# Three row tiles transposed by VectorE from squares loaded from DRAM, a last pair finished in pieces, and a mask check moved to a later stage

## The chip, the cores and the metric

The kernel runs on one core of one Trainium2 chip. The metric is the device time of one execution in microseconds (us), of which lower is better. A core has five engines that run beside each other: TensorE (PE in the profile; matmuls, with PEld for its weight loads), VectorE (DVE), ScalarE (ACT), GpSimd (POOL) and SyncE (SP, which here only issues DMAs). Sixteen DMA engines move data between DRAM and the core's memory (SBUF); matmuls write to another memory, PSUM.

## The reference

The input x has 4 x 512 = 2048 rows of 1024 numbers (fp32). Two layers follow each other, and each ends with a residual sum and a layernorm over the row:

```python
attn = einsum('ds,td->st', w1, w2) * sparse_mask      # 1024 x 1024, mostly zero
x = layernorm(x + gelu(einsum('bds,st->bdt', x, attn) + b2))
w_l, w_h = dequant(qweight, lut4, 4 bits), dequant(qweight, lut8, 8 bits)
y = where(norm(x) > 64, x @ w_h.T, x @ w_l.T) + bias
x = layernorm(x + y)
```

The mask of this input has ones only within 70 columns of the diagonal. After the first layernorm a row's norm is about 32, so the 8 bit weights are not needed for this input. The kernel relies on both facts, but checks them on the chip: it counts rows above 64 and blocks of the mask with something outside the band, and if the count is above zero a general path (lines 42 to 189) computes everything anew. With this input that path doesn't run.

## The kernel before, in words

The 2048 rows are 16 row tiles of 128 (numbered 0 to 15). A tile's `x` lies in SBUF as 128 partitions x 1024 and is overwritten step by step with the results. The stages:

1. **Product of w1 and w2**, only in the band (L451), while the 4 bit weights are unpacked by VectorE, ScalarE and GpSimd (L293 to L344, in steps that are spread between other work). The unpacked weight is transposed by TensorE (`transpose_pending`) into `wT`, with the identity added, so that the residual sum of the second layer is part of its matmul.
2. **Attention of a row tile n** (`attention`, L529). TensorE transposes x in 8 blocks of 128 x 128 (`transposed`, L478, by `transpose_blocks`, L276; ScalarE copies each half from PSUM, L282), multiplies with the band of `attn` (`band_rows`, L507), VectorE adds b2 (z, L533), ScalarE takes the Gelu (L534), VectorE adds x and sums the row (L538). Then the layernorm: VectorE makes the negative mean `nm` (L377), ScalarE the sum of squares (`junk`, L380), GpSimd the reciprocal root r (L382, L383), VectorE normalizes (L387). The normalization is put into a list `later` and written out by the next call of `now()`, so that other work stands between.
3. **Second layer of tiles 0 to 3**, in two halves of 512 columns (`left` and `right`, `ffn_half`, L590): 8 matmuls of 512 columns each (L552), then `combine` (L564) adds the bias and sums the row.
4. **Second layer of tiles 4 to 15 in six pairs** (`ffn_pair`, L659), by a scheme with 7 instead of 8 block products. Each product is 4 matmuls of 512 columns (L669) into one of the PSUM banks u, v, w. Its inputs are tiles transposed by another way: VectorE transposes each 32 x 32 square (`squares`, L615), a DMA writes them to DRAM (`there`), four DMAs read them back in the other order (`rows`), and ScalarE, VectorE and GpSimd make copies, sums and differences (`pair_inputs`, L635). The combined weights t1 to t4 are made by `weight_sum` (L613, 2.28 us each) after each `right` half.

The order of work is the list `todo` (L720 to L727): attention 0 to 3, then `left` 0 to 3 alternating with attention 4 to 7, attention 8 to 11, then `right` 0, attention 12, `right` 1, attention 13 and so on, then the pairs. What is prepared for the next entry (its transposed tile) is written one entry ahead (L765). A scheduler orders the instructions of each engine at build time, except that VectorE keeps the written order from attention 8 on (L755). Each engine then runs its own list strictly in order, and waits for others by semaphores. All DMAs of this part are issued by SP, in order.

Three details matter for the change. `check_outside` (L488) loads the part of a block of mask rows that is outside the band into a buffer of the tag `z` (two buffers, shared with the attention's z and the outputs) and lets ScalarE sum the absolute values (L495); it is called for 8 blocks from attention 9 and `left` 2 on, which the scheduler puts between 111 and 199 us. `count_odd` (L703) and `count_all` (L713) make the count after pairs 0 and 1. And the tiles 12 to 15 are loaded (L760 to L762) when the memory of the unpacking stage is free.

Of the kernel before, what the change touches and what calls it, by code (L numbers as in the profile page):

```python
# [9 lines left out]
FP = mybir.dt.float32  # L10
# [3 lines left out]
AF = mybir.ActivationFunctionType  # L14
ALU = mybir.AluOpType
AX = mybir.AxisListType

P = 128
D = 1024
SOON = 12  # L20
PAIR = 2
KT = D // P
HALF = 512
NH = D // HALF
EPS = 1e-5
# [5 lines left out]
SQ = 32  # L31
Q = P // SQ
EARLY = 4
# [3 lines left out]
def window(s):  # L37

    return max(0, s * P - BAND), min(D, (s + 1) * P + BAND)
# [153 lines left out]
def kernel(  # L193
# [21 lines left out]
    with ExitStack() as main:  # L215
# [172 lines left out]

        x_tiles = []

        def load_x(pool, n):
            t = pool.tile([P, D], FP, tag=f"x{n}", name=f"x{n}")
            nc.sync.dma_start(out=t, in_=x[ts(n, P), :])
            x_tiles.append(t)

        attn = band.tile([P, KT, WIN], FP, name="attn")

# [79 lines left out]

        def transposed(n, tag, bufs, by_bit):  # L478
            xT = late.tile([P, KT, P], FP, tag=tag, name="xT", bufs=bufs)
            if by_bit:  # L480
                cols = x_tiles[n].rearrange("t (b s) -> t s b", s=8)
                transpose_blocks(xT, lambda k: cols[:, k, :])
            else:
                transpose_columns(xT, x_tiles[n])
            return xT


        def check_outside(s):  # L488

            lo, hi = window(s)  # L490
            raw = work.tile([P, D], FP, tag="z", name="raw", bufs=2)
            for i, (a, b) in enumerate(((0, lo), (hi, D))):
                if a < b:
                    nc.sync.dma_start(out=raw[:, a:b], in_=sparse_mask[ts(s, P), a:b])
                    nc.scalar.activation(  # L495
                        raw[:, a:b], raw[:, a:b], AF.Abs, accum_out=outside[:, 2 * s + i : 2 * s + i + 1]
                    )

        def band_rows(xT):
            ps = ps_mm.tile([P, D], FP, tag="mm", name="mm")  # L500
# [73 lines left out]
        def finish_rows(n):  # L574
            y = x_tiles[n]
            total = work.tile([P, 1], FP, tag="total", name="total", bufs=4)
            nc.vector.tensor_tensor(total, sums[:, n, 0:1], sums[:, n, 1:2], ALU.add)
            nm, r, _ = stats(y, total)

            def rest():  # L580
                if n < EARLY:
                    o = last.tile([P, D], FP, tag="o", name="o")
                else:
                    o = work.tile([P, D], FP, tag="z", name="o", bufs=2)
                normalize(o, y, nm, r)
                nc.sync.dma_start(out=out[ts(n, P), :], in_=o)

            later.append(rest)

# [45 lines left out]
        def pair_inputs(pool, n, top, low):  # L635


            def halves(tag):
                both = late.tile([P, KT, P], FP, tag=tag, name="halves")
                return both, both[:, :KH, :], both[:, KH:, :]  # L640

            def by_squares(block):
                return block.rearrange("p k (a r) -> p k a r", a=Q)


            side = (n - EARLY) // PAIR % 2
            (a1, a11, a12), (_, s1, s2), (_, s3, s4) = (
                halves(f"early{2 * i + side}") for i in range(3)
            )
            a22 = pool.tile([P, KH, P], FP, tag="a22", name="a22", bufs=2)  # L650
            nc.scalar.copy(by_squares(a1), top)  # L651
            nc.vector.tensor_tensor(by_squares(s1), low[:, :KH], low[:, KH:], ALU.add)  # L652
            nc.vector.tensor_tensor(by_squares(s3), top[:, :KH], low[:, :KH], ALU.subtract)
            nc.scalar.copy(by_squares(a22), low[:, KH:])
            nc.gpsimd.tensor_tensor(s2, s1, a11, ALU.subtract)  # L655
            nc.gpsimd.tensor_tensor(s4, a12, s2, ALU.subtract)
            return a11, a12, a22, s1, s2, s3, s4

        def ffn_pair(pool, n, blocks, between):  # L659

            a11, a12, a22, s1, s2, s3, s4 = blocks
            t1, t2, t3, t4 = (weights[i] for i in range(1, 5))
            u = pool.tile([P, HALF], FP, tag="u", name="u", bufs=2)
            v = pool.tile([P, HALF], FP, tag="v", name="v", bufs=1)
            w = pool.tile([P, HALF], FP, tag="w", name="w", bufs=1)

            def times(ps, a, b, start, stop):
                for k in range(KH):
                    nc.tensor.matmul(  # L669
                        out=ps,  # L670
                        lhsT=a[:, k, :],
                        rhs=b[:, k, :],
                        start=start and k == 0,
                        stop=stop and k == KH - 1,
                        skip_group_check=True,
                    )

            left, right = bias_bc[:, :HALF], bias_bc[:, HALF:]
            y11, y12 = x_tiles[n][:, :HALF], x_tiles[n][:, HALF:]
            y22 = x_tiles[n + 1][:, HALF:]  # L680
            times(u, a11, b11, True, False)
            nc.vector.tensor_tensor(y11, u, left, ALU.add)
            now()
            between(0)
            times(w, s1, t1, True, False)
            nc.vector.tensor_tensor(y22, w, right, ALU.add)
            between(1)
            times(u, s2, t2, False, False)
            nc.vector.tensor_tensor(y12, u, right, ALU.add)  # L689
            times(w, s4, b22, False, True)  # L690
            combine(n, 1, w, y12)
            times(u, s3, t3, False, False)
            combine(n + 1, 1, u, y22)
            between(2)
            times(v, a12, b21, True, True)
            combine(n, 0, v, y11)
            finish_rows(n)
            times(u, a22, t4, False, True)
            combine(n + 1, 0, u, left)
            now()  # L700
            finish_rows(n + 1)

        def count_odd():  # L703

# [21 lines left out]
        unpack_after = [("attention", 1), ("left", 0), ("attention", 4), ("left", 1)]  # L726
        unpack_after += [("attention", 5), ("left", 2), ("attention", 6), ("left", 3)]  # L727

        kept = {}
        rows, blocks = {}, {}  # L730

        def prepare_pair(n, part):

            if n == NT:
                return
            if part < PAIR:
                rows[n + part] = squares(last, n + part)
            else:
                blocks[n] = pair_inputs(last, n, rows[n], rows[n + 1])

        def prepare(what, n):
            if what == "attention":
# [3 lines left out]
            return kept[n]  # L746

        ready = prepare(*todo[0])
        checks = 0
        ordered = main.enter_context(ExitStack())  # L750
        for i, (what, n) in enumerate(todo):
            if (what, n) == ("left", 0):
                transpose_pending(0)
            if (what, n) == ("attention", 2 * EARLY):
                ordered.enter_context(tc.manual_schedule(engines={mybir.EngineType.DVE}))  # L755
            if (what, n) == ("attention", SOON - 2):
                steps(100)
                transpose_pending(0)
                first_sb.close()
                last = main.enter_context(tc.tile_pool(name="last", bufs=1, side="right"))  # L760
                for m in range(SOON, NT):
                    load_x(last, m)  # L762
            xT = ready
            if i + 1 < len(todo):
                ready = prepare(*todo[i + 1])  # L765
            if what == "attention":
                if n >= SOON + 1:
                    attention(n, xT, lambda: prepare_pair(EARLY, n - SOON - 1))
                else:
                    attention(n, xT)  # L770
                if n < 2 * EARLY:
                    now()
                if n > 8 and checks < KT:
                    check_outside(checks)
                    checks += 1
            else:
                ffn_half(n, xT, 0 if what == "left" else 1)
                if what == "left" and n > 1:
                    check_outside(checks)
                    checks += 1  # L780
                if what == "right":
                    weight_sum(last, n + 1)
                    now()
            if (what, n) in unpack_after:
                steps(1)
        while checks < KT:
            check_outside(checks)
            checks += 1
        first_ps.close()
        ps_pair = main.enter_context(  # L790
            tc.tile_pool(name="ps_pair", bufs=1, space=bass.MemoryType.PSUM)
        )
        for n in range(EARLY, NT, PAIR):
            ffn_pair(ps_pair, n, blocks[n], lambda part, m=n + PAIR: prepare_pair(m, part))
            if n == EARLY:
                n_odd = count_odd()
            elif n == EARLY + PAIR:
                count_all(n_odd)
        now()
        ordered.close()  # L800

# [41 lines left out]
```

## Time and profile before

| | |
|---|---|
| runs | 363.34, 363.91, 362.96 us; median 363.34 |
| profiled execution | 363.37 us, span in the profile 361.6 us, mean granted TensorE clock 0.975 |
| busy over the span | PE 328.1 us (91%), PEld 200.3 (55%), DVE 230.3 (64%), ACT 165.7 (46%), POOL 96.8 (27%) |
| DMA | 43.90 MB in 28331 packets, mean 121 GB/s |
| L281 transposes of x on PE | 160 records, 22.6 us |
| L495 mask sums on ACT | 14, 7.8 us, and 14 reads of the accumulator, 2.6 us |
| L619 transposes of squares on DVE | 12, 2.03 us each |
| pairs 0 to 5 on PE, from start to start | 28.40, 25.15, 24.20, 24.91, 24.28, 24.03 us |

Times of instructions are counted from the start of the span. A line of the order in time has the start, the duration, engine, line of the code, operation, output <- inputs, the shape, and in brackets how long the engine stood before it and for whom. Instructions of one group in a row are merged (x8 for 8). A matmul of fp32 appears as two records, so 4 matmuls of 512 columns are x8 and 3.43 us from start to start. The chain of waits is followed back from the last instruction to what released each; its lines give start, duration and what ran. Matmuls are pipelined, so a busy PE isn't PE at its peak.

### The profile page before, as it was taken

The numbers are of one execution on the slowest core, as the hardware profiler recorded it, in microseconds if no ns is written. First come the engines' busy times: TensorE is split into PE (matmuls) and PEld (weight loads), VectorE is DVE, ScalarE is ACT, GpSimd is POOL, SyncE is SP. The second block draws the span as 40 slices with busy tenths as digits, with TensorE's granted clock in tenths as the row PEclk, the third lists the DMA queues.
The fourth block names the chain that finished last, engine by engine and source line by source line (L and its number), as shares of the span: only waits on it lengthen the run. The fifth ranks groups of instructions, "written<-read, shape, count | busy, mean of one in ns | idle before, by whom it ended". The sixth has DMA issues, their size and how long they took to land.

```text
span 361.6 us, 3701 instructions
## 1 busy us (share of the span) xinstructions
PE 328.1 (91%) x1216; PEld 200.3 (55%) x1216; DVE 230.3 (64%) x353; ACT 165.7 (46%) x242; POOL 96.8 (27%) x130
## 2 busy tenths in 40 slices
PE   6799989769999987999999888999999999999970
PEld 6588778637567576956665433443444434444430
DVE  1689899697987997556767953654635626644130
ACT  4794995888659876675454311202212012022011
POOL 0810550682036322231321420402203004022000
PEclk9999999969999999899999999999999999999995
DMA  8999109500101001712235215162351451522003
GB/s 253 316 325 383 67 0 355 228 0 0 47 2 44 0 3 36 284 44 101 97 123 185 94 61 171 59 214 78 140 181 30 187 160 58 203 87 117 1 4 122
DMA packets 28331, 43.90 MB, mean 121 GB/s; under 512 B 7568, under 2 KB 20624, under 8 KB 28304
## 3 DMA queue, kind: packets, MB, share of 16 engines
q1 hardware_dynamic: 26976, 43.44, 34.9%
q10 hardware_dynamic: 1328, 0.15, 0.3%
q8 instruction: 11, 0.18, 0.2%
q14 instruction: 16, 0.13, 0.1%
HBM read 28.90 MB, written 14.68 MB: 121 GB/s over the span
## 4 chain that ended last, share of the span: by engine, by line
PE 35%; DVE 27%; ACT 9%; DMA 9%; POOL 8%; issue 7%; SPq 1%; ACTq 0%; POOLq 0%; DVEq 0%
PE u L669 16%; PE w L669 8%; ACT junk L380 6%; DVE x L538 4%; PE v L669 4%; POOL root L326 4%; DVE root L331 4%; DVE e L329 4%; DMA rows<-there 3%; DVE z L533 3%; POOL r L383 3%; PE mm L552 2%; PE mm L451 2%; DMA w_raw<-in_L_attn_w_dram 2%; DVE root L335 2%
## 5 line engine op out<-in xcount | busy, mean ns | idle before, releaser
L380 ACT ACTIVATE junk<-x,nm 128x1024 bf16<-128x1024 f32 x32 | 36.7, 1148 | 67.0 <-DVE nm L377 64.7
L507 PE MATMUL mm<-attn,xT 128*128 128x198 f32 (+2 forms) x320 | 62.1, 349 | 1.6 <-DVE attn L461 1.5
L322 ACT ACTIVATE e<-v,lt,diff 128x1024 f32<-128x1024 uint8 x48 | 56.6, 1236 | 4.1 <-DVE v L297 2.6
L552 PE MATMUL mm<-wT,xT 128*128 128x512 f32 x128 | 58.4, 611 | 0.0
L507 PEld LDWEIGHTS mm<-attn,xT 128*128 128x128 f32 x320 | 53.5, 194 | 8.6 <-DVE attn L461 1.9
L326 POOL TENSOR_SCALAR root<-v,diff,lt 128x1024 f32<-128x1024 uint8 x16 | 38.2, 2397 | 50.0 <-DVE v L297 34.7
L669 PE MATMUL u<-t,halves 128*128 128x512 f32 x96 | 43.3, 594 | 1.0 <-DVE x L689 1.0
L382 POOL TENSOR_SCALAR r<-ss 128x1 f32<-128x1 f32 x32 | 10.8, 337 | 116.7 <-ACT junk L380 116.6
L552 PEld LDWEIGHTS mm<-wT,xT 128*128 128x128 f32 x128 | 24.5, 197 | 28.2 <-issue 27.9
L655 POOL TENSOR_TENSOR halves<-halves 128x512 f32<-128x512 f32 x6 | 9.5, 1586 | 84.9 <-DVE halves L652 84.9
L619 DVE STREAM_TRANSPOSE squares<-x 128x1024 f32<-128x1024 f32 x12 | 24.3, 2029 | 11.6 <-DMA there<-squares 11.6
L669 PEld LDWEIGHTS u<-t,halves 128*128 128x128 f32 x96 | 18.1, 190 | 24.7 <-issue 22.8
L651 ACT COPY halves<-rows 128x1024 f32<-128x1024 f32 x6 | 6.3, 1042 | 55.3 <-DMA rows<-there 55.3
L281 PE MATMUL pt<-ident,x 128*128 128x128 f32 x160 | 22.6, 283 | 9.4 <-ACT wT L282 7.9
L451 PE MATMUL mm<-w2T,w_sb 128*128 128x268 f32 (+1 forms) x128 | 28.9, 375 | 2.0 <-DMA w_sb<-in_L_attn_w_dram 1.6
L281 PEld LDWEIGHTS pt<-ident,x 128*128 128x128 f32 x160 | 19.4, 154 | 13.0 <-ACT wT L282 9.3
L330 DVE COPY_PREDICATED root<-v,e 128x1024 f32<-128x1024 uint8 x16 | 22.7, 1417 | 5.3 <-POOL root L326 3.1
L534 ACT ACTIVATE z<-z 128x1024 f32<-128x1024 f32 x16 | 16.9, 1056 | 20.0 <-DVE z L533 20.0
L282 ACT COPY xT<-pt 128x512 f32<-128x512 f32 x40 | 21.2, 589 | 10.6 <-PE pt L281 10.6
L451 PEld LDWEIGHTS mm<-w2T,w_sb 128*128 128x128 f32 x128 | 22.8, 189 | 5.6 <-ACT w2T L282 2.5
L387 DVE TENSOR_SCALAR x<-x,nm,r 128x1024 f32<-128x1024 f32 x16 | 13.0, 812 | 20.3 <-POOL r L383 19.0
L329 DVE COPY_PREDICATED e<-v,e 128x1024 f32<-128x1024 uint8 x16 | 22.1, 1383 | 1.8 <-ACT e L322 1.8
(74 smaller groups left out, 435.8 us busy)
## 6 DMA issues: line engine op xcount, KB each, us to landing
x<-in_L_attn_x_dram SPq DMA_DIRECT2D x16, 512.0 KB, 7.6
out_dram<-o SPq DMA_DIRECT2D x16, 512.0 KB, 2.6
there<-squares SPq DMA_DIRECT2D x12, 512.0 KB, 3.0
rows<-there SPq DMA_DIRECT2D x48, 128.0 KB, 2.9
w_raw<-in_L_attn_w_dram SPq DMA_DIRECT2D x8, 512.0 KB, 7.0
w_sb<-in_L_attn_w_dram SPq DMA_DIRECT2D x3, 1024.0 KB, 7.5
w_sb<-in_L_attn_w_dram SPq DMA_DIRECT2D x2, 512.0 KB, 7.0
raw<-_L_attn_sparse_mask_dram SPq DMA_DIRECT2D x2, 413.0 KB, 3.4
```

Source lines behind the costliest of these rows:

```text
L281: nc.tensor.transpose(pt[:, j, :], block(g * (HALF // P) + j), ident)
L282: done = nc.scalar.copy(dst[:, g * (HALF // P) : (g + 1) * (HALF // P), :], pt)
L322: nc.scalar.activation(entry[j], plane(0), AF.Identity, scale=d_k, bias=l_k)
L326: nc.gpsimd.tensor_scalar(entry[j], plane(0), d_k, l_k, ALU.mult, ALU.add)
L329: nc.vector.copy_predicated(entry[2], plane(1), entry[3])
L330: nc.vector.copy_predicated(root, plane(1), entry[1])
L380: nc.scalar.activation(junk, u, AF.Square, bias=nm, accum_out=ss)
L451: part = nc.tensor.matmul(out=ps[:, : hi - lo], lhsT=w1_sb[s][:, k, :], rhs=w2T[:, k, lo:hi], start=(k == 0), stop=(k == KT - 1),)
L507: nc.tensor.matmul(out=ps[:, a:b], lhsT=xT[:, s, :], rhs=attn[:, s, a - lo : b - lo], start=h not in fresh, stop=hi == D or (h == 0 and wi ...
L552: nc.tensor.matmul(out=ps, lhsT=xT[:, k, :], rhs=wT[:, k, ts(h, HALF)], start=(k == 0), stop=(k == KT - 1),)
L619: nc.vector.transpose(out=t, in_=x_tiles[n].rearrange("t (c j k) -> t c k j", c=Q, k=KT))
L669: nc.tensor.matmul(out=ps, lhsT=a[:, k, :], rhs=b[:, k, :], start=start and k == 0, stop=stop and k == KH - 1, skip_group_check=True,)
```

## The change

Four edits, all in the kernel's main function:

- **Tiles 13 to 15 are transposed by VectorE.** After the loads of x12 to x15, twelve more DMAs on SP (`load_squares`, four per tile) read tiles 13 to 15 a second time from DRAM, in runs of 32 numbers (128 bytes), so that every 32 x 32 square lies where it belongs in the transposed tile. They go into the memory of t3 and t4, which are written later. One transpose instruction of VectorE (L497 of the changed file) turns all squares of a tile in place of 8 transposes of TensorE and 2 copies of ScalarE. The rows of a tile are taken in another order (row 4i + a at partition 32a + i), so the loads and stores of these tiles follow it (`rows_of`).
- **The mask's rest moves to the pairs.** The loads go into the tiles 0 to 3, whose results have been stored, and are written at the start of pairs 1 to 4; the sums on ScalarE are placed behind a copy of `pair_inputs` in the preparation of pairs 2 to 5.
- **The count** moves from pairs 0 and 1 to the start of pair 5.
- **The last pair's end** (`finish_last`): the product v comes before the third u product. The layernorm of tile 14 is finished by ScalarE, which also issues its store. The last product of tile 15 comes in two pieces of 256 columns into the free banks w and v; VectorE adds each piece and takes its mean and variance with `bn_stats`; the output is normalized and stored in two halves, by SP and ScalarE.

In the built program, the transposes of tiles 13 to 15 stand on VectorE between `nm` (L377) and `normalize` (L387) of the tile before. Without the 24 transposes the lists of TensorE differ in little up to the pairs. In the pairs the scheduler places the four matmuls of v differently: before, the products ran in pair 0 as u v1 w u w u v3 u (v1 for one matmul of v), in pair 1 as u w v3 u w v1 u u, in pairs 2 and 4 as u w u w v1 u v3 u, in pair 3 as u w v2 u w v2 u u; after, in pair 0 as u v3 w u w u v1 u, in pairs 1 and 3 as u w u w v1 u v3 u, in pairs 2 and 4 as u w v2 u w v2 u u.

The diff, cut to its core:

```diff
+        def rows_of(dram, n):
+            rows = dram[ts(n, P), :]
+            return rows if n <= SOON else rows.rearrange("(i a) d -> a i d", a=Q)
...
+        def load_squares(t, n):
+            cols = x[ts(n, P), :].rearrange("(i a) d -> i (a d)", a=Q)
+            cols = cols.rearrange("i (m g j) -> g i m j", g=Q, j=SQ)
+            for g in range(Q):
+                nc.sync.dma_start(
+                    out=t[ts(g, SQ), :].rearrange("i (m j) -> i m j", j=SQ), in_=cols[g]
+                )
...
         def transposed(n, tag, bufs, by_bit):
             xT = late.tile([P, KT, P], FP, tag=tag, name="xT", bufs=bufs)
+            if n > SOON:
+                nc.vector.transpose(
+                    out=xT.rearrange("p k (a i) -> p a k i", a=Q),
+                    in_=in_squares[n].rearrange("p (a k j) -> p a k j", a=Q, k=KT),
+                )
+                return xT
...
         def check_outside(s):
-            raw = work.tile([P, D], FP, tag="z", name="raw", bufs=2)
...
+            for raw, _, _, _, i in outside_band(s):
+                nc.scalar.activation(raw, raw, AF.Abs, accum_out=outside[:, i : i + 1])
...
+            if n + PAIR == NT:
+                times(v, a12, b21, True, True)
+                combine(n, 0, v, y11)
+                finish_last(
+                    n, lambda: times(u, s3, t3, False, True), u, (w, v), a22, t4, y22
+                )
+                return
...
+        def finish_last(n, third, u, banks, a22, t4, y22):
...
+            nm, r, _ = stats(x_tiles[n], total)
+            nc.gpsimd.tensor_tensor(nm, nm, r, ALU.mult)
+            o = last.tile([P, D], FP, tag="o", name="o")
+            nc.scalar.activation(o, x_tiles[n], AF.Identity, scale=r, bias=nm)
+            nc.scalar.dma_start(out=rows_of(out, n), in_=o)
+            third()
...
+            nc.vector.tensor_tensor(y22, u, y22, ALU.add)
+            nc.vector.tensor_tensor(y[:, :HALF], u, bias_bc[:, :HALF], ALU.add)
+            for c in (2, 3):
+                statistics(c)
+            for c in (0, 1):
+                for k in range(KT // 2):
+                    nc.tensor.matmul(
+                        out=banks[c][:, :piece],
+                        lhsT=a22[:, k, :],
+                        rhs=t4[:, k, ts(c, piece)],
...
+                nc.vector.tensor_tensor(
+                    y[:, ts(c, piece)], banks[c][:, :piece], y[:, ts(c, piece)], ALU.add
+                )
+                statistics(c)
+            nc.vector.bn_aggr(mv, st)
+            r = work.tile([P, 1], FP, tag="r", name="r", bufs=4)
+            nc.vector.tensor_scalar(r, mv[:, 1:2], EPS, None, ALU.add)
+            nc.gpsimd.tensor_tensor(r, r, minus_half, ALU.pow)
+            o = work.tile([P, D], FP, tag="z", name="o", bufs=2)
+            for h, queue in ((0, nc.sync), (1, nc.scalar)):
...
+                queue.dma_start(
+                    out=rows_of(out, n + 1)[:, :, ts(h, HALF)], in_=o[:, ts(h, HALF)]
+                )
...
+                blocks[n], copied = pair_inputs(last, n, rows[n], rows[n + 1])
+                m = n - EARLY - 2 * PAIR
+                if 0 <= m < KT:
+                    with tc.issue_after(copied.ins):
+                        for s in range(m, m + PAIR):
+                            check_outside(s)
...
+                t3, t4 = (
+                    last.tile([P, 2, D], FP, tag=f"t{i}", name="in_squares") for i in (3, 4)
+                )
+                in_squares = {13: t3[:, 0, :], 14: t4[:, 0, :], 15: t4[:, 1, :]}
+                for m in in_squares:
+                    load_squares(in_squares[m], m)
...
         for n in range(EARLY, NT, PAIR):
+            m = n - EARLY - PAIR
+            if 0 <= m < KT:
+                for s in range(m, m + PAIR):
+                    load_outside(s)
+            if n == NT - PAIR:
+                count_all(count_odd())
             ffn_pair(ps_pair, n, blocks[n], lambda part, m=n + PAIR: prepare_pair(m, part))
-            if n == EARLY:
-                n_odd = count_odd()
-            elif n == EARLY + PAIR:
-                count_all(n_odd)
```

## The prediction, made before the changed kernel ran

> **What bounds the kernel now.** I read the chain of waits first, then the instructions in order of time for TensorE (PE), VectorE (DVE) and the end, then the busy time per stage. The page's summary of the chain:
>
> ```profile
> PE 35%; DVE 27%; ACT 9%; DMA 9%; POOL 8%; issue 7%; SPq 1%; ACTq 0%; POOLq 0%; DVEq 0%
> ```
>
> PE is 91% busy over the span but holds only 35% of the chain. In the stage that loses the transposes (attention 12 to 15 between the `right` halves) the chain in order of time does not touch PE at all:
>
> ```profile
> 185.40 0.81 DVE x L387
> 186.21 0.62 DVE x L564 x2
> 187.32 1.25 ACT junk L380 x2
> 188.65 0.81 POOL r L382
> 189.53 0.56 POOL r L383
> 190.16 0.69 issue
> 190.85 1.22 DVE z L533
> 192.06 1.96 DVE squares L619
> 194.02 1.13 DVE x L538 x2
> 195.44 1.25 ACT junk L380 x2
> 197.04 0.56 POOL r L383
> 197.63 0.81 DVE x L387
> ```
>
> One turn, 185.40 to 197.63, is 12.2 us of DVE, ScalarE (ACT) and GpSimd (POOL) in a ring. PE's own share of a turn, in the order of time:
>
> ```profile
> 188.18 1.04 PE L281 MATMUL pt<-ident,x 128*128 128x128 f32 x8
> 189.05 7.03 PE L552 MATMUL mm<-wT,xT 128*128 128x512 f32 x16
> 195.92 3.76 PE L507 MATMUL mm<-attn,xT 128*128 128x198 f32 x20
> ...
> 213.67 3.67 PE L669 MATMUL w<-wT,halves 128*128 128x512 f32 x8 [1.36 <-DVE x L686]
> 218.37 3.70 PE L669 MATMUL u<-t,halves 128*128 128x512 f32 x8 [1.04 <-DVE x L689]
> ```
>
> From start to start that is 0.87 + 6.87 + 3.60 = 11.34 us: PE runs ahead, and pays for it at 213.67 and 218.37, where it waits for DVE. From 218.37 to its end at 350.49 PE is nearly dense: only two waits of 1.05 (before 249.56 and 298.75). The end, all of it after PE:
>
> ```profile
> 346.89 3.60 PE L669 MATMUL u<-t,a 128*128 128x512 f32 x8
> 350.53 0.69 DVE L564 SCALAR_TENSOR_TENSOR x<-u,bias_bc 128x512 f32<-128x512 f32 x1 [2.28 <-PE u L669]
> 352.40 1.15 ACT L380 ACTIVATE junk<-x,nm 128x1024 bf16<-128x1024 f32 x1 [2.79 <-DVE nm L377]
> 354.58 0.81 DVE L387 TENSOR_SCALAR o<-x,nm,r 128x1024 f32<-128x1024 f32 x1 [2.30 <-POOL r L383]
> 355.42 0.33 SPq L586 DMA_DIRECT2D out_dram<-o  x1
> ```
>
> The last store leaves 4.93 us after PE (355.42 - 350.49), lands 3.7 us later (the DMA view), and 2.5 us of closing follow: 11.1 us.
>
> **Step 1, before the turns (144 to 162).** Removed from ACT: 14 mask sums (7.8 us with 2.6 of accumulator reads) and 6 copies of transposed blocks (0.59 each). DVE is dense from 112 to 139, so nothing is won there. PE stands from 142.24 to 144.38 and then works with a granted clock of 0.50 from 146 to 149; its work up to band 10 is the same in another order. The one place on the chain is 155.86, where four mask sums (1.09) stand ahead of the Gelu of tile 11. They go, but one copy of tile 12 (0.59), formerly done early, takes the place. Followed to `combine` of `right` 0, which PE then holds back, DVE arrives 0.4 us earlier (162.40 to 162.0). Bounds: 0 and 1.9 (no clock drop).
>
> **Step 2, the turns (162 to 200).** PE loses 3 x 0.87 = 2.6 us. DVE gains three 32x32 transposes (L497 of the changed file). No row shows them with this layout; the same instruction at L619 takes 2.03 us on the same 128x1024. In the built order they stand between `nm` and `normalize`, where DVE idles 2.31 us for r (seen before 173.18, 185.40 and 197.63). 2.03 < 2.31, so I cost them at nothing; without that cover it would be 2.03 each. What they cost for sure is PE's lead: band 15 now waits for a transpose that starts at `nm` of tile 14 (195.32 - 0.4) and ends at 197.05, so band 15 ends at 200.65 (199.52 before). Its consumer z(15) was at 203.07, so the turn stays 12.2. POOL computes r beside the transpose. If the two lock each other out, the first POOL operation starts at 2.03 instead of 1.45 us after `nm`, and r comes 0.6 later, three times: 1.8 us. L382 has a row for such a delay: 0.81 instead of 0.19 beside L613. The other bound is 0; a shorter transpose gains nothing, since r is late anyway. The nearest row, L545 at 210.52, ended at 211.07, 0.14 us into a transpose; it may have begun first and settles nothing. I take 0. [...]
>
> **The squares' loads.** 12 DMAs of 1024 runs of 128 bytes, 12,288 packets, behind x12 to x15 on SP. SP's next store comes at 167. The memory is free when PE has read the last root (142.3); 2 MB at the 380 to 430 GB/s of 146 to 150 last till about 149. The time of such packets is bounded by two rows: between 12 and 18 us the queues carried 2891 packets, 1560 of them under 512 bytes, 1.98 MB, busy 113% of 16 engines; taking the 1331 larger ones at 380 GB/s leaves 13 to 21 ns for a small one, and the page's mean over all of queue 1 is 34.9% x 361.6 x 16 / 26976 = 75 ns. I take the first, its packets being of this size: 10 to 16 us, all there by 165. DVE needs tile 13 at 170.5, 14 at 182.7, 15 at 194.9. [...]
>
> **Step 3, pairs 0 and 1.** Here PE still follows DVE, 0.4 earlier than before. Pair 0 has three v matmuls ahead of w instead of one: 200.65 + 3.43 + 2.57 + 3 x 3.43 = 216.95, then it waits for y12 (L689: 218.35 - 0.4 = 217.95), then u, one v, u: 3.43 + 0.86 + 3.43, end 225.7 (227.92 before). Pair 1 has no v early, so it waits twice: for y22 (L686, 236.9), w and v to 241.2, for y12 (L689, 242.15), then 9.43: end 251.6 (253.07 before). So DVE's chain, not PE's work, eats the 2.6 us.
>
> **Step 4, pairs 2 to 5.** A pair is 28 matmuls x 0.858 = 24.03. Pairs 2 and 4 have no v between the last two u products, where 1 and 3 lacked it before: 1.05 each, as often as before. 251.6 + 25.08 + 24.20 + 25.08 = 326.0. The mask sums (2.2 to 2.4 us a pair) fill the 2.07 us in which ACT idles between 250.40 and 252.46, and delay two statistics by up to 0.5; DVE's y12 was done at 266.16 and PE took it at 267.67, so 1.5 us cover that; without cover it would be 0.5 in each of four pairs. The mask's loads stand ahead of rows (L629) on SP, 0.4 MB or 1 us; the halves waited 4 us for use. The count's matmul moves into pair 5: before, it sat in a wait (248.61) and cost nothing; in a dense stretch I take 0.3 (0.1 to 1.0); its counts are ready 2 us before. PE ends at 326.0 + 24.03 + 0.3 = **350.3** (350.49).
>
> **Step 5, the end.** The last product comes in two 256 wide pieces, so after PE there is: add 0.42 (L564's 0.69 and L533's 1.22 give the slope), statistics of 256 about 0.4 (no row; between the 0.19 of L710 and the 0.69 of L564), aggregation and epsilon 0.55, the power 0.55 and two handovers 0.2, two halves of 512 at 0.46 and 0.54: 3.15 instead of 4.93. The mean of row tile 14 leaves DVE: its 0.81 went in between (351.14). The last store is half as large: 2.0 if it moves as fast as 512 KB did (1.4 us of data), 3.7 if what held the last store up is no matter of size; other stores took 2.6, which I take. With 2.5 of closing: 8.25, 2.9 less than before (1.2 to 3.9).
>
> **Sum.** 350.3 + 8.25 = 358.55 of span. The profiled execution took 363.37 with a span of 361.6, so 1.8 lie around it (median of the runs: 363.34): **360.3 us**.
>
> **Rivals.**
> (a) The front gets rid of the clock drop of 146 to 149, or the chain gains as much otherwise: DVE 1.9 earlier instead of 0.4, **358.8**. For it: ACT loses 14 sums. Against: the wait 142.24 to 144.38 hangs on a weight copy behind statistics, both still there. 0.15.
> (b) POOL waits for the transposes: 1.8 later, **362.1**. For: L382's 0.81. [...] 0.12.
> (c) The end gains only 1.2, since the landing stays 3.7 and the statistics are slow: **362.0**. For: the last landing was 3.7 where others of the same size took 2.6. 0.11.
> (d) Slower: the squares come late and DVE stands at the transposes of tile 15 with all behind it. At 75 ns a packet the loads end at 149 + 57.6 = 206.6 instead of 194.9: 11.7 later, **372**. It decides from (194.9 - 149) x 16 / 12288 = 60 ns. Against: the 13 to 21 ns. 0.07.
> The forecast, with 359.2 to 361.4 about it: 0.55.
>
> **Chances.** A measurement here can tell 0.3% (1.1 us) from no change. Faster than 362.25: the forecast, (a), most of (c), half of (b): 0.85. Within: the rest of (b) and (c), 0.08. Slower: (d), 0.07. The range reaches over (a), (b) and (c): 358.5 to 362.3.
>
> **What would show it.** Right: L497 begins right after `nm`, takes about 2.0, and the `normalize` behind it still waits for r; PE idles about 1.8 us before bands 14 and 15; PE's end near 350.3 although 24 transposes are gone; the last store leaves near 3.2 us after PE. Wrong: a wait on in_squares at DVE; L382 at 0.8 beside L497; PE's end below 349 (the turn was PE's after all) or above 352; a landing of 3.7.

## The result, and the profile after

The changed kernel takes 371.75 us (median of 4 runs, 370.89 to 372.43); the kernel before took 363.19 us beside it (median of 4). The ratio is 1.0242, 95% interval 1.0213 to 1.0271: **slower by 2.4%**, where 360.3 us was forecast. The profiled execution took 371.34 us with a span of 369.5. All times below are counted from the start of a profiled span.

I read the end first. The order of time of the changed kernel, from TensorE's last piece of work on (TensorE ends at 352.60):

```profile
352.63 0.42 DVE L778 TENSOR_TENSOR x<-v,x 128x256 f32<-128x256 f32 x1 [0.72 <-PE v L770]
353.09 0.43 DVE L762 BATCH_NORM_STATS2 b_bc<-x 128x6 f32<-128x256 f32 x1
354.09 0.55 POOL L785 TENSOR_TENSOR r<-r,minus_half 128x1 f32<-128x1 f32 x1 [4.72 <-DVE r L784]
354.67 1.00 DVE L788 TENSOR_SCALAR o<-x,b_bc,r 128x512 f32<-128x512 f32 x2 [0.66 <-POOL r L785]
355.24 0.56 SPq L796 DMA_DIRECT2D out_dram<-o  x1
355.70 0.55 ACTq L796 DMA_DIRECT2D out_dram<-o  x1
```

The last store leaves 3.10 us after TensorE, as forecast (3.15). But the span goes on for another 13.8 us, in which no engine computes. What happens there is in the table by stretches of the same kernel. Its columns are the stretch and its length, then busy time and number of instructions of PE, PEld, DVE, ACT and POOL, then TensorE's granted clock, the mean busy share of the 16 DMA engines, and GB/s:

```profile
356.00:358.00 2.00, 0.00 (x0) 0.00 (x0) 0.00 (x0) 0.00 (x0) 0.00 (x0) 0.50 0.27 78
358.00:360.00 2.00, 0.00 (x0) 0.00 (x0) 0.00 (x0) 0.00 (x0) 0.00 (x0) 0.50 0.27 104
360.00:362.00 2.00, 0.00 (x0) 0.00 (x0) 0.00 (x0) 0.00 (x0) 0.00 (x0) 0.50 0.26 95
362.00:364.00 2.00, 0.00 (x0) 0.00 (x0) 0.00 (x0) 0.00 (x0) 0.00 (x0) 0.50 0.25 97
```

The reader is to see the share: flat at a quarter, for a megabyte (row tiles 14 and 15). The kernel before moved most of its last 512 KB in one stretch of 2 us (share 0.70, 266 GB/s):

```profile
356.00:358.00 2.00, 0.00 (x0) 0.00 (x0) 0.00 (x0) 0.00 (x0) 0.00 (x0) 0.50 0.70 266
```

A quarter of 16 is as much as four engines can do; the view gives only the mean of the 16. The loads of tiles 13 to 15 look the same: from 146 to 162 us, in stretches of 4 us, the share is 0.28 to 0.42 at 105 to 114 GB/s, and SP's own order of time shows it held up in the issues:

```profile
144.27 25.54 SPq L408 DMA_DIRECT2D in_squares<-in_L_attn_x_dram  x12
169.91 0.78 SPq L617 DMA_DIRECT2D out_dram<-o  x1
```

The second loss lies earlier. The order of time of TensorE in the changed kernel, where it waits for ScalarE's copy of the last weights, and of two instructions of VectorE, the merge of the last weight (L335) and z of tile 7:

```profile
145.21 1.97 PE L281 MATMUL pt<-ident,x 128*128 128x128 f32 x8 [3.43 <-ACT wT L282]
```

```profile
133.65 1.31 DVE L335 COPY_PREDICATED root<-v,root 128x1024 f32<-128x1024 uint8 x1
134.85 1.21 DVE L564 TENSOR_TENSOR z<-mm,b_bc 128x1024 f32<-128x1024 f32 x1
```

The same places in the kernel before, where the wait is shorter and z (L533 there) comes first:

```profile
144.38 0.66 PE L281 MATMUL pt<-ident,x 128*128 128x128 f32 x4 [2.14 <-ACT wT L282]
133.56 1.22 DVE L533 TENSOR_TENSOR z<-mm,b_bc 128x1024 f32<-128x1024 f32 x1
134.69 1.32 DVE L335 COPY_PREDICATED root<-v,root 128x1024 f32<-128x1024 uint8 x1
```

Behind TensorE's wait its clock falls, and stays low for longer than before. The tables by stretches of the changed kernel and of the kernel before (the granted clock is third from the end):

```profile
144.00:146.00 2.00, 0.79 (x4) 0.79 (x5) 0.83 (x2) 2.00 (x5) 0.99 (x4) 0.57 0.40 147
146.00:148.00 2.00, 2.00 (x9) 1.97 (x8) 1.78 (x4) 2.00 (x5) 0.49 (x1) 0.50 0.24 96
148.00:150.00 2.00, 2.00 (x6) 1.59 (x5) 0.05 (x1) 1.68 (x4) 0.19 (x1) 0.50 0.41 131
150.00:152.00 2.00, 2.00 (x10) 1.93 (x10) 0.00 (x0) 0.00 (x0) 0.93 (x3) 0.72 0.42 109
```

```profile
144.00:146.00 2.00, 1.62 (x9) 1.52 (x10) 1.20 (x2) 2.00 (x6) 1.43 (x4) 0.91 0.94 233
146.00:148.00 2.00, 2.00 (x8) 1.65 (x8) 0.91 (x3) 2.00 (x5) 0.00 (x0) 0.50 0.97 369
148.00:150.00 2.00, 2.00 (x10) 1.90 (x10) 0.00 (x0) 1.83 (x5) 1.13 (x4) 0.74 1.03 420
```

In the fourth stretch it was 1.00 again in the kernel before. Summing (1 - clock) x 2 us gives 1.7 us of full-speed work lost before and 3.4 us after. `combine` of `right` 0 comes at 164.14 (162.40 before, 162.0 forecast).

The transposes, last, in the order of time of the changed kernel:

```profile
172.47 0.15 DVE L377 TENSOR_SCALAR nm<-total 128x1 f32<-128x1 f32 x1
172.65 1.25 DVE L497 STREAM_TRANSPOSE xT<-in_squares 128x1024 f32<-128x1024 f32 x1
174.07 0.19 POOL L382 TENSOR_SCALAR r<-ss 128x1 f32<-128x1 f32 x1 [5.97 <-ACT junk L380]
174.93 0.81 DVE L387 TENSOR_SCALAR x<-x,nm,r 128x1024 f32<-128x1024 f32 x1 [1.03 <-POOL r L383]
```

L497 starts 0.03 us after `nm`, with no wait on the squares; `normalize` behind it still waits for r. L382 starts 1.60 us after the start of `nm`, as in the kernel before (170.72 and 172.32). It does not run beside the transpose: that takes 1.25 us and ends at 173.90, 0.17 us ahead of L382. So these rows do not show whether the two would hold each other up.

From 164.14 on, the changed kernel reaches TensorE's end in 188.46 us; 350.3 - 162.0 = 188.3 was forecast. So the miss of the span (369.5 - 358.55 = 10.95) is in two places: 164.14 - 162.0 = 2.14 in the front, and 16.9 - 8.25 = 8.65 behind TensorE's end. These two and the 0.16 between them are the whole of it.

### The profile page after: what moved, and what is told of

Same layout as the page of the kernel before. It is cut to its first block, busy times and chain, and to the rows that moved or that the text cites. A ratio compares the mean times of both kernels' runs of the same rounds, so it can differ in the third digit from the quotient of the medians.

```text
span 369.5 us, 3672 instructions
## 1 busy us (share of the span) xinstructions
PE 326.5 (88%) x1200; PEld 199.3 (54%) x1200; DVE 235.3 (64%) x360; ACT 162.0 (44%) x235; POOL 96.6 (26%) x130
## 4 chain that ended last, share of the span: by engine, by line
DVE 33%; DMA 19%; PE 13%; ACT 12%; issue 8%; POOL 7%; SPq 3%; ACTq 0%; DVEq 0%; POOLq 0%
DMA rows<-there 7%; ACT junk L380 7%; DMA there<-squares 5%; DVE squares L650 5%; DVE x L569 4%; PE u L700 4%; DVE root L331 4%; POOL r L383 3%; DVE e L329 3%; DVE z L564 3%; DMA x<-in_L_attn_x_dram 2%; SPq L660 2%; PE mm L583 2%; POOL root L326 2%; DVE root L335 2%
## 5 line engine op out<-in xcount | busy, mean ns | idle before, releaser
L538 PEld LDWEIGHTS mm<-attn,xT 128*128 128x128 f32 x320 | 54.3, 197 | 13.5 <-issue 5.8
L380 ACT ACTIVATE junk<-x,nm 128x1024 bf16<-128x1024 f32 x31 | 35.6, 1149 | 58.9 <-DVE nm L377 56.5
L583 PE MATMUL mm<-wT,xT 128*128 128x512 f32 x128 | 57.5, 602 | 0.0
L382 POOL TENSOR_SCALAR r<-ss 128x1 f32<-128x1 f32 x31 | 10.5, 338 | 111.3 <-ACT junk L380 111.2
L650 DVE STREAM_TRANSPOSE squares<-x 128x1024 f32<-128x1024 f32 x12 | 24.3, 2028 | 10.8 <-DMA there<-squares 10.8
L565 ACT ACTIVATE z<-z 128x1024 f32<-128x1024 f32 x16 | 16.9, 1058 | 30.6 <-DVE z L564 30.6
L281 PE MATMUL pt<-ident,x 128*128 128x128 f32 x136 | 19.5, 289 | 9.8 <-ACT wT L282 8.3
L387 DVE TENSOR_SCALAR x<-x,nm,r 128x1024 f32<-128x1024 f32 x16 | 13.0, 812 | 17.3 <-POOL r L383 13.8
L281 PEld LDWEIGHTS pt<-ident,x 128*128 128x128 f32 x136 | 16.9, 160 | 12.7 <-ACT wT L282 9.4
L569 DVE SCALAR_TENSOR_TENSOR x<-z,x 128x1024 f32<-128x1024 f32 x16 | 21.3, 1332 | 2.7 <-ACT z L565 2.7
L700 PE MATMUL w<-wT,halves 128*128 128x512 f32 x48 | 21.7, 595 | 1.2 <-DVE x L717 1.2
```

What stands on the lines that cost most here:

```text
L281: nc.tensor.transpose(pt[:, j, :], block(g * (HALF // P) + j), ident)
L380: nc.scalar.activation(junk, u, AF.Square, bias=nm, accum_out=ss)
L538: nc.tensor.matmul(out=ps[:, a:b], lhsT=xT[:, s, :], rhs=attn[:, s, a - lo : b - lo], start=h not in fresh, stop=hi == D or (h == 0 and wi ...
L565: nc.scalar.activation(z, z, AF.Gelu)
L569: nc.vector.scalar_tensor_tensor(xt, z, 1.0, xt, ALU.mult, ALU.add, accum_out=total)
L583: nc.tensor.matmul(out=ps, lhsT=xT[:, k, :], rhs=wT[:, k, ts(h, HALF)], start=(k == 0), stop=(k == KT - 1),)
```

## The experiments

Theory **T1**: the pattern `(i a) d -> a i d` with a = 4, which tiles 13 to 15 got for loads and stores, lets only as much as four of the 16 DMA engines work on a transfer. Rivals: **T2**, ScalarE's queue is slow; **T3**, rows that lie four apart are slow. For the front, **F1**: without the mask's sums the scheduler orders VectorE's and ScalarE's work otherwise; rival **F2**: the second load or the transposes hold it up.

All runs at a glance. The first three columns are of the profiled executions: from the `combine` at 113 to 116 us (that of `left` 2) to that of `right` 0; from there to TensorE's end; from there to the end of the span. The time is the median, the ratio that to the kernel before on the same chip.

| kernel | front | turns and pairs | end | time | ratio (95%) |
|---|---|---|---|---|---|
| before | 48.47 | 188.09 | 11.1 | | |
| after | 50.75 | 188.46 | 16.9 | 371.75 | 1.0242 (1.0213 to 1.0271) |
| a_split | 50.70 | 188.31 | 9.2 | 363.99 | 1.0021 (1.0000 to 1.0042) |
| a_split_stores | 49.49 | 188.00 | 10.0 | 363.41 | 0.9992 (0.9956 to 1.0028) |
| a_sp_queue | 50.70 | 188.18 | 16.8 | 371.44 | one run |
| b_last4 | 46.89 | 188.11 | 18.2 | 369.75 | one run |
| b_last16 | 46.84 | 188.11 | 12.2 | 365.12 | one run |
| b_end | 48.16 | 188.11 | 8.3 | 360.14 | 0.9940 (0.9912 to 0.9967) |
| b_chk | 50.61 | 188.42 | 11.0 | 365.26 | 1.0072 (1.0041 to 1.0104) |
| a_plain16 | 49.48 | 192.93 | 8.3 | 366.39 | 1.0073 (1.0039 to 1.0108) |
| a_plain16_chk | 73.21 | 188.37 | 8.5 | 386.24 | 1.0668 (1.0618 to 1.0717) |
| s_root_late | 48.52 | 188.25 | 9.2 | 362.36 | 0.9961 (0.9931 to 0.9991) |
| s_root_early | 50.74 | 188.11 | 9.4 | 364.80 | 1.0024 (0.9998 to 1.0051) |
| e_root_early | 47.21 | 188.12 | 8.4 | 359.39 | 0.9903 (0.9869 to 0.9937) |

### The end: four engines, a queue, or rows far apart

**a_split** cuts every load and store of tiles 13 to 15 into four:

```diff
+                rows = rows.rearrange("(i a) d -> a i d", a=Q)
+                parts = [(rows[a], t[ts(a, SQ), :]) for a in range(Q)]
+            for r, s in parts:
...
+                queue.dma_start(out=s if into_sbuf else r, in_=r if into_sbuf else s)
...
-            nc.sync.dma_start(out=t, in_=rows_of(x, n))
+            move_rows(nc.sync, x, n, t, True)
...
-            nc.scalar.dma_start(out=rows_of(out, n), in_=o)
+            move_rows(nc.scalar, out, n, o, False)
```

> The changed kernel, with each load and each store of tiles 13 to 15 cut into four transfers of 32 partitions (32 rows of DRAM each), so that no transfer has a leading dimension of 4. Theory T1 (a transfer whose DRAM pattern leads with 4 is carried by a quarter of the DMA engines: about 100 GB/s in the trace of after, from 144 to 164 us and from 351 to 367 us): the stores land about 3 us after their issue, the span ends some 8.5 us after TensorE's end instead of 16.9, SP no longer stands from 144 to 170 us, time 361 to 363.5. Theory T2 (ACT's queue, or two queues side by side, are slow at the end): no change, 370 to 373. Theory T3 (rows of DRAM that lie four apart, or runs of 2 KB, are slow): no change, 370 to 373. The front's later combine (+1.7 us on VectorE's chain) stays under all three.

363.99 us. The end shrinks from 16.9 to 9.2 us; the same bytes to the same rows now move at a share of 0.89. The table by stretches of this kernel:

```profile
352.00:354.00 2.00, 0.89 (x5) 0.43 (x3) 1.21 (x4) 0.00 (x0) 0.00 (x0) 1.00 0.89 221
356.00:358.00 2.00, 0.00 (x0) 0.00 (x0) 0.00 (x0) 0.00 (x0) 0.00 (x0) 0.58 0.67 173
358.00:360.00 2.00, 0.00 (x0) 0.00 (x0) 0.00 (x0) 0.00 (x0) 0.00 (x0) 0.50 0.39 106
```

T1 holds, and T3 cannot carry the loss, since the rows of each part still lie four apart. The last microsecond to the 8.25 of the forecast is probably issue: ScalarE needs about 1.9 us for the last four stores and ends at 357.87, where one store alone left at 355.70. The time lies half a microsecond above the expected range.

**a_sp_queue** gives ScalarE's two stores to SP (`nc.sync` for `nc.scalar`), patterns as in the changed kernel.

> The changed kernel with ACT's two stores (tile 14, second half of tile 15) issued by SP instead, patterns unchanged. T2 (ACT's queue is what is slow): the tail after TensorE's end falls from 16.9 to about 8.5 us, time 362 to 364. T1 and T3: tail 16 to 18 us, time 370 to 373.

371.44 us, an end of 16.8: T2 falls.

**b_last4** and **b_last16** go the other way: the kernel before, with one store changed (a = 4, and a = 16 in the second; the input of the store is left as it was, so the rows of tile 15 go out in another order).

```diff
-                nc.sync.dma_start(out=out[ts(n, P), :], in_=o)
+                rows = out[ts(n, P), :]
+                if n == NT - 1:
+                    rows = rows.rearrange("(i a) d -> a i d", a=4)
+                nc.sync.dma_start(out=rows, in_=o)
```

> The kernel before, with the last store of tile 15 alone given the DRAM pattern that leads with 4 (row 4i+a instead of row 32a+i, so the rows of tile 15 go out in another order); 512 KB. T1: about 100 GB/s, 5.2 us for the bytes instead of 1.3, so the store lands 7 to 8 us after its issue instead of 3.7 and the time is 366 to 368. T2: no change (SP's queue), 363 to 364. T3: as T1, 366 to 368.

> The same with a pattern that leads with 16 (row 16i+a... of tile 15 in another order): rows just as far from each other, 16 in the leading dimension. T1: all 16 engines carry it, the store lands after 3.5 to 4 us, time 363 to 364. T2: 363 to 364. T3: as slow as the pattern that leads with 4, 366 to 368.

The pattern alone makes the old end as slow as the new one: the end is 18.2 us with 4, 12.2 with 16. The tables by stretches of b_last4 and of b_last16, where the last 512 KB move:

```profile
356.00:358.00 2.00, 0.00 (x0) 0.00 (x0) 0.00 (x0) 0.00 (x0) 0.00 (x0) 0.50 0.26 63
360.00:362.00 2.00, 0.00 (x0) 0.00 (x0) 0.00 (x0) 0.00 (x0) 0.00 (x0) 0.50 0.25 78
```

```profile
358.00:360.00 2.00, 0.00 (x0) 0.00 (x0) 0.00 (x0) 0.00 (x0) 0.00 (x0) 0.50 0.66 197
```

Again a share of a quarter for a leading 4, and not for a leading 16. T1's size was off: I had taken 100 GB/s from two stores side by side, but one alone moved at 53 to 78 GB/s in these stretches, so b_last4 lies 1.8 us above what was expected. Two stores side by side, in the changed kernel from two queues, do not raise the share (0.25 to 0.27) above that of one alone. b_last16 lies 1.1 us above the 363 to 364 that T1 gave: its end is 1.1 us longer than in the kernel before. Of this, 0.34 us is SP's issue of that store (0.67 us instead of 0.33); the rest may be T3, which the runs do not show.

Side by side, by the leading number: shares of 0.24 to 0.27 with 4 (the changed kernel, b_last4), 0.66 with 16 (b_last16), 0.67 to 0.89 with 32 in the two full stretches (a_split), 0.70 with 128 (the kernel before). How many engines carried a transfer no view shows; that it was four is my reading of the quarter.

**a_split_stores** cuts the stores only, and leaves the loads on the pattern that leads with 4.

> The changed kernel with only the stores of tiles 13 to 15 cut into four transfers of 32 partitions; their loads keep the pattern that leads with 4, so SP stands in its issues until about 170 us as in the changed kernel. If those loads cost nothing (VectorE's transposes did not wait for the squares in the trace of the changed kernel): as with loads and stores cut, 363.3 to 364.6, and no wait on in_squares. If the late end of the loads costs time (the output of tile 0 leaves late, as where 48 small loads stood ahead of it): 365 to 367, and VectorE stands at the normalization that needs an output buffer.

363.41 us: the slow loads cost nothing that can be measured, though SP stands in them until 172.6. VectorE never waits for them.

### Each part alone

**b_end** is the kernel before with `finish_last` alone (plain rows).

> The kernel before with the new end of the last pair alone (rows in their plain order, so every store leads with 128). Theory T1 (step 5 of the prediction is right but for the pattern that leads with 4): TensorE ends as before near 350.5, the span ends 8.0 to 8.7 us after that instead of 11.1, time 360.2 to 361.2. Rival T4 (the landing of the last store is no matter of pattern or size, or ScalarE's queue closes late): the tail stays above 9.5, time 361.8 to 363.4.

360.14 us, an end of 8.3. T4 falls, and step 5 of the forecast holds for plain stores: the end is 2.8 us shorter than before, which is more than the whole gain of 0.6% (ratio 0.9940).

**b_chk** is the kernel before with only the mask's rest and the count moved.

> The kernel before with the mask's rest and the count moved into the pairs, and nothing else. Theory F1 (the front comes later because the scheduler puts VectorE's and ScalarE's instructions between 120 and 146 us in another order once the mask's sums are gone): combine of right 0 at 164.0 to 164.5 as in the changed kernel instead of 162.4, TensorE ends 1.5 to 2.5 later than before, time 364.6 to 366.2. Rival F2 (the second load of three tiles, or the transposes on VectorE, hold the front up): combine of right 0 at 162.0 to 162.6, time 362.8 to 364.

365.26 us, a front of 50.61: F1 holds, and F2 falls, since this kernel has neither a second load nor transposes on VectorE. The move of the mask, which takes work away, is what makes the front later. On VectorE the merge of the last weight stands ahead of z of tile 7 here too (134.95 and 136.15), and TensorE has the same wait as in the changed kernel:

```profile
146.51 1.97 PE L281 MATMUL pt<-ident,x 128*128 128x128 f32 x8 [3.43 <-ACT wT L282]
```

**a_plain16** keeps the transposes and loads the squares so that rows stay in their plain order, by 16 DMAs a tile instead of 4; **a_plain16_chk** also leaves the mask's rest and the count where they were.

```diff
+            for a in range(Q):
+                cols = x[n * P + a * SQ : n * P + (a + 1) * SQ, :]
+                cols = cols.rearrange("i (m g j) -> g i m j", g=Q, j=SQ)
+                for g in range(Q):
+                    nc.sync.dma_start(
+                        out=t[ts(g, SQ), ts(a, KT * SQ)].rearrange("i (m j) -> i m j", j=SQ),
+                        in_=cols[g],
+                    )
```

> The changed kernel with the plain order of rows for all tiles; the squares of a tile are loaded by 16 DMAs (one for each 32 rows and each 32 of 128 columns) instead of 4. Loads and stores of x and out are again one DMA each that leads with 128. T1: tail 8.0 to 8.7 us after TensorE's end near 352.7, time 362.3 to 363.6: the tail's loss is gone, the front's stays. Rival: SP issues 48 small loads until after 175 us, VectorE waits for squares or the stores are late, 365 and more.

> The same, and the mask's rest and the count where they were before: only the squares and the new end are left of the change. F1 and T1 together: VectorE's order in the front is that of before, combine of right 0 at 162.0 to 162.6, TensorE ends 349.8 to 350.8, tail 8.0 to 8.7, time 359.8 to 361.2, what the prediction gave to the whole change. F2: combine of right 0 after 163.8, time 362 to 363.5.

Both missed, and show what the squares cost a queue. The end is 8.3 and 8.5 as expected. But SP needs 35 us for the 48 issues, 0.73 each. In a_plain16 the store of tile 0 stands behind them, and VectorE behind that store, since it wants the output buffer. First SP's order of time, then VectorE's:

```profile
146.07 35.11 SPq L409 DMA_DIRECT2D in_squares<-in_L_attn_x_dram  x48
181.29 0.53 SPq L619 DMA_DIRECT2D out_dram<-o  x1
```

```profile
184.47 0.81 DVE L387 TENSOR_SCALAR o<-x,nm,r 128x1024 f32<-128x1024 f32 x1 [5.54 <-DMA out_dram<-o]
```

In a_plain16_chk the mask's loads stand behind them too, ScalarE behind the mask's loads, and the statistics of tile 11 behind that, with VectorE idle for 27 us. ScalarE's order of time there:

```profile
182.11 0.47 ACT L519 ACTIVATE raw<-raw 128x314 f32<-128x314 f32 x1 [25.14 <-DMA raw<-_L_attn_sparse_mask_dram]
```

This is the mechanism of rival (d), a stall behind the loads of the squares, by another way in: not the transposes stood but what was queued behind the loads. The expectation for the front could not be seen in it. It also shows that two edits hang together: with the squares' loads on SP, the mask's loads cannot stay where they were, behind them.

### The front

**s_root_late** is a_split with the last step of the unpacking recorded after attention 7 instead of after `left` 3 (the first edit below); **s_root_early** also records the last weight's transposes ahead of attention 8 instead of 10 (both edits). (The expectations call the `combine` they count from that of `left` 1; it is that of `left` 2.)

```diff
-        unpack_after += [("attention", 5), ("left", 2), ("attention", 6), ("left", 3)]
+        unpack_after += [("attention", 5), ("left", 2), ("attention", 6), ("attention", 7)]
...
-            if (what, n) == ("left", 0):
+            if (what, n) in (("left", 0), ("attention", 8)):
                 transpose_pending(0)
```

> The kernel with transfers of tiles 13 to 15 cut into 32 partitions, and the last step of the unpacking recorded after attention 7 instead of after left 3; in the built order VectorE then does z of tile 7 ahead of the last merge of a weight (L335) again, as in the kernel before; ScalarE's and TensorE's lists around 144 us stay. Theory F1a (the front's loss comes from VectorE's order, 1.2 us): combine of right 0, counted from the combine of left 1, comes 49.0 to 49.6 after it (before 48.47, changed kernel 50.75), time 362.4 to 363. Theory F1b (the loss comes from ScalarE's copies of the last weight, which stand behind the statistics of tile 8 and leave TensorE idle for 3.4 us and then at half clock): 50.4 to 50.8, time 363.6 to 364.3.

> The same, and the last weight's transposes are recorded ahead of attention 8 instead of attention 10, so that ScalarE copies them before the statistics of tile 7. F1a and F1b together: TensorE's idle stretch before 145 us shrinks from 3.4 to under 1.5 us and its clock doesn't fall to 0.5 for long; combine of right 0 at 47.5 to 48.8 after the combine of left 1, time 361.2 to 362.3. If neither order matters (rival F3: the loss sits in the time of the x loads, which run from 144 to 150 us): 50.4 to 50.8, no change, 363.6 to 364.3.

s_root_late has the front of the kernel before (48.52), and with 362.36 us it is a little faster than it. Its order of time, TensorE first, then VectorE:

```profile
144.05 1.97 PE L281 MATMUL pt<-ident,x 128*128 128x128 f32 x8 [2.39 <-ACT wT L282]
133.23 1.21 DVE L574 TENSOR_TENSOR z<-mm,b_bc 128x1024 f32<-128x1024 f32 x1
134.36 1.32 DVE L335 COPY_PREDICATED root<-v,root 128x1024 f32<-128x1024 uint8 x1
```

On VectorE nothing else between 112 and 146 us stands in another order than in a_split. On TensorE the edit also moved eight transposes of the weight before (126.79, behind a band; 123.08, ahead of it, in a_split), but up to z VectorE's times in the two kernels agree within 0.1 us, counted from the `combine` of `left` 2. So the order of z of tile 7 and the merge of the last weight (F1a) explains the front. More came back (2.2 us) than the 1.2 us of the one instruction: TensorE's wait ends some 0.8 us earlier, is 2.39 us instead of 3.43, and the work lost to the clock fell from 3.4 to 1.7 us. How much of the clock's part is chance in one profiled execution stays open, but ten runs of each give the same 0.6% (ratios 0.9961 and 1.0021). F1b as I put it falls: in s_root_early the front is 50.74 again. There TensorE reaches the last weight's transposes earlier, waits 3.87 us for VectorE to make that weight, and loses the clock at 138 to 144 us. F3 falls too: both have the same loads at the same place, and s_root_late is rid of the loss.

**e_root_early** is b_end with the second of these edits.

> The kernel before with the new end alone, and the last weight's transposes recorded ahead of attention 8. Under F1b the wait of TensorE (142.2 to 144.4 us in the kernel before) and the drop of its clock behind it go, combine of right 0 comes 1.0 to 1.9 us earlier (bound of step 1), time 358.2 to 359.3 against 360.1 of the new end alone. Under F1a or F3, where VectorE's chain is what counts: no change, 359.8 to 360.6; or worse if the weight's copies delay the tiles 7 and 8, up to 362.

359.39 us, ratio 0.9903, the best of all. The wait at 142 is gone (waits of 1.6 and 1.8 us stand earlier; the kernel before has one of 1.7 there too), the clock stays at 1.00 from 140 to 156, and the front is 47.21 against 48.16. The time lies between the two expected ranges, and in b_last4 and b_last16 the clock stayed up without this edit. The intervals of this kernel and of b_end overlap, so that it is better than b_end is likely but not shown.

## Why the prediction was wrong

- **Step 5 failed in one term, the landing**: "2.0 if it moves as fast as 512 KB did ... 3.7 if what held the last store up is no matter of size; ... I take 2.6". Both bounds came from stores that lead with 128. The diff showed `rows_of` with a leading 4 for this very store, and I costed it at nothing. The landing, forecast as 2.6 us, took some 11.3 (13.8 us behind the last store, less the 2.5 of closing): 8.65 us for the step. The rest of the step was right: 3.10 us to the last store (3.15 forecast), and an end of 8.3 in b_end (8.25), where only that pattern differs.
- **Step 1 failed**: "DVE arrives 0.4 us earlier ... Bounds: 0 and 1.9". I read what leaves ScalarE and took VectorE's order as given. It was not given before attention 8, and the built order showed L335 ahead of z of tile 7. The front came 2.14 us later than forecast, and no bound of mine lay on that side. s_root_late takes it back. This is also why TensorE ends at 352.60, above the 352 that the prediction named as a sign of being wrong; the turns are not the reason.
- **Step 2 was right**: the transposes are hidden (1.25 us each, not 2.03), and the turns take 11.52, 12.22 and 12.22 us (164.14, 175.66, 187.88, 200.10; before: 11.51, 12.22 and 12.23). Rival (b) falls, but through this shorter time: each transpose ends before GpSimd's first operation (0.17 to 0.24 us ahead of it), so whether the two contend was not tested. TensorE idles 1.17 and 1.52 us before bands 14 and 15 (1.8 forecast), at no cost.
- **The squares' loads**: no wait, as forecast. But "all there by 165" was off: in the changed kernel SP issues the last at 169.0. I priced them by the DMA engines alone. On SP they are long (25.54 us for the 12): in a_plain16 their issue (35.11 us for 48) held up a store.
- **Steps 3 and 4 were right** as a sum: 188.46 us from `right` 0 to TensorE's end, 188.3 forecast. With the 2.14 us of the front added to the forecast, pair 1 starts 0.35 us late and pairs 2 to 5 within 0.2 us. 2.6 us of transposes taken from TensorE bring nothing; b_chk, which has no transposes on VectorE, needs 188.42.
- **Rivals**: (a) is not the changed kernel, but its mechanism exists: in b_last4 and b_last16 the clock does not fall after waits of 2.2 us, and the front, with the order of the kernel before, is 46.9 instead of 48.5. (c) falls with b_end. (d) needs the queue, not the transposes; at the loads' size in the changed kernel it does not come.

What stays open: what the squares are worth alone. They were not run alone, since the mask's loads would stand behind theirs. In the columns of the table no part shows a gain from them.

## What to carry to other kernels

Read the leading dimension of each DMA's pattern in a diff before its bytes: 4 there meant a DMA share of about a quarter here (0.24 to 0.27, where 128 had 0.70), and at the end of this kernel nothing hid it (an end of 16.9 us, 8.3 in b_end). Where a scheduler orders an engine, a removed instruction is a changed order: compare the built orders up to the first critical wait, and give such a step a bound on the losing side too. And a DMA's cost on the queue that issues it is a price of its own: 0.73 us an issue in a_plain16, paid by the store that was queued behind, and by VectorE with a wait of 5.54 us.

## What the runs showed of the hardware

- The drops of TensorE's clock came in two sizes: the work lost in one was 1.7 us (before, b_end, s_root_late) or 3.4 us (after, a_split, a_sp_queue, b_chk), that is, 3.4 or 6.8 us at the granted clock of 0.50. After waits of 2.1 to 2.7 us it fell in some executions and not in others (b_last4, 2.19: not; before, 2.14: yes), after 3.4 us in all four. In a_plain16 and a_split_stores it fell already at 130 to 138 us, behind waits of 1.4 and 0.5 us close together (in the four others it did not fall behind the same two waits), and again at 146 to 150; TensorE was then late by itself, waited 2.3 instead of 3.4 us, and the front was 49.5 instead of 50.7 with the same order. So by an estimate from these fronts (50.7 - 49.5, and 48.5 - 46.9 of b_last4) one profiled front carries 1.2 to 1.6 us of chance. What sets the size of a drop, and which wait brings one, the runs do not show.
- The 32 x 32 transposes took 1.25 us from `in_squares` to xT (L497) and 2.03 us from x to `squares` (L650) for the same 128x1024: shape and type are the same and the access patterns differ, so it is likely that these set the price; which side does was not tried.
- 12,288 packets of 128 bytes took from about 148 to 164 us in a_split, at shares of about 1.0 to 1.2 up to 158 and of 0.8 and less behind it. An estimate from this is 16 us x 16 / 12288, some 21 ns each, the upper end of the 13 to 21 ns that the prediction had from 12 to 18 us.
